# GAT blocks in a written order with their logits in PSUM, PSUM operands in the slot stage, and a fence between one-hots and GIN

## The chip, the core and the metric

The kernel runs on one core of one Trainium2 chip. Its metric is the time of one execution on the device in microseconds (us); the median of three runs is given. A run under the hardware profiler gives the trace and has a time of its own.

The core has five engines that run their own queues of instructions in order: PE (matrix multiplication; its weight loads are shown as PEld), DVE (VectorE), ACT (ScalarE), POOL (GpSimd) and SP (here only a queue that issues DMAs). They meet through semaphores. SBUF and PSUM are the memories on the chip[...].

## The reference

3125 nodes with 64 features and 103,125 edges, sorted by destination. Two parts, each added to its input:

```python
h = jnp.maximum(_layernorm(x, axis=-1), 0.0)
x = x + _L0_gnn_ref(h, edge_index, edge_weight, ...)    # GIN
h = jnp.maximum(_layernorm(x, axis=-1), 0.0)
x = x + _L1_gnn_ref(h, edge_index, node_vec, ...)       # GAT
```

The GIN part has three layers; the sums over edges are weighted:

```python
agg = jax.ops.segment_sum(x[src] * ew[:, None], dst, num_segments=x.shape[0])
h = jax.nn.relu((agg + x) @ w1 + b1) @ w2 + b2
```

The GAT part adds a time embedding (two dense layers over sines and cosines of `noise_labels`), and has three layers of 8 heads, of width 256, 256 and 128; per layer a softmax over the edges of each destination, a batch normalization, a parallel dense path and a SiLU:

```python
logits = leaky_relu(al_s[src] + al_d[dst], 0.2)         # [edges, 8]
e = jnp.exp(logits - segment_max(logits, dst)[dst])
alpha = e / segment_sum(e, dst)[dst]
out = segment_sum(alpha[:, :, None] * xw[src], dst)     # + bias
x = silu(batchnorm(out + x @ aw + ab))
```

A dense layer to 64 features ends it. All is fp32.

## The kernel before

Nodes are handled in NT = 25 tiles of P = 128 (NP = 3200). If a flag computed on the chip allows it, the path of class `Fast` runs, as here. Its stages, with lines of the kernel:

- `search` (L623) and `rank` (L711) find the row of edges of each destination and sort destinations by degree, so that each tile t of destinations has its own number of edge slots, `CAPS[t]` (64 down to 23, 857 in all). ACT's queue zero-fills the dense matrix `adj` in DRAM (40.96 MB).
- `slots` (L749). Its inner `weigh(t)` (L817) compares all pairs of a destination's slots to add up double edges: the wide operations L824 (`same`), L827 (`part`, with the fixed triangle `earlier` of L812), L828 (a sum), L833 and L834. `put(t)` (L836) writes slot columns into `adj`, one indirect DMA on POOL for each column (L943): 857 of them, in the order tiles 0 to 2, 3 to 7, then 50 scatters of tables, then tiles 8 to 24. Under these run, on DVE, the compares L866 and L869 with the maximum L870, which pick for each destination and each tile of sources at most one edge (`tops`, later `lane`), a series of match and maximum operations for the edges left over (`row`, at most 44 for a destination, `MORE[t]` per block t of 128), a second `rank`, and the flag.
- `fast` (L1290): layer norm, the embedding `embed` (L154; its `em_t` loads are on SP, its first DVE operation is L175, its last copy on ACT L188), `hots` (L923) and then three `gin` (L954). `hots` makes for each of 25 tiles a one-hot of the chosen edges: the comparison L929 of `lane` and `iota` on DVE, 25 transposes on PE, copies on ACT (L938), and a store of 800 KB on SP (L939).
- `gin` reads the whole of `adj` (122.9 MB over three layers) in 225 loads on SP (L973, eight buffers), and multiplies on PE (L977).
- `gat` (L991) three times. Its first part makes the transformed features in three bf16 parts (`split`), the attention terms and the dense path. `add_edges` (L1058) is the largest stage of the kernel, and has a loop over the 25 tiles. For each step t:
  - `gather(t+1, ...)` (L1071): 26 slots for each destination (25 from the one-hots `hot`, loaded on SP, and the node itself), by 78 bf16 matmuls into PSUM tiles `g`, two slots in each, copied by ACT into `rows` (L1079). It works in three parts, of 12, 12 and 2 slots.
  - `add_part` (L1102) on the three parts of tile t: `times` multiplies by `e` on DVE (L1100), the second half of the slots is added onto the first (L1105), and 6+6+1 matmuls with the identity add up the rest on PE into `pa1` (L1107). Then a copy on ACT (L1163) and a store.
  - where they are due (L1165), blocks of left-over edges: `others` (L1111) fetches on POOL a row `at` and `MORE[k]` rows `rows` from DRAM (L950, six buffers of 8 rows), and lets POOL scatter the result of an earlier block into `more` (L943). `add_others` (L1125) makes logits (L1128), `lrelu` (L206), exponentials (`exps`, L1180 to L1183, the exponential itself on ACT L1182), `times`, identity matmuls (L1139) and a copy (L1140).
  - `weigh(t+1)` (L1085): logits of the next tile's 26 slots (L1088, L1092), `lrelu`, `exps`.
- `close_rows` (L1185) joins the parts, with batch norm; `finish` (L278) ends the kernel.

The language's scheduler decides the order of each engine's queue from its own estimates; the order of the text is a starting point, not the result. It also places the semaphores. Pools of buffers (`bufs`) decide how far a producer may run ahead. In PSUM there is one pool `gat_ps` for a whole layer, with two buffers for most names.

## Time and profile before

| what | us |
|---|---|
| median of three runs | 5105.78 (5102.36 to 5115.34) |
| profiled execution, own time | 5023.04 |
| its span, first to last instruction | 5021.1 |
| puts into `adj`, first to last | 243 to 1497 |
| GIN with what stands beside it | 1503 to 1922 |
| GAT loops, layers 0, 1, 2 | 1003, 1004, 692 |
| between and around them | 90, 133, 114, 63 |
| busy: PE, DVE, ACT, POOL | 2248.5, 2020.8, 862.4, 2677.6 |
| mean granted TensorE clock | 0.729 |

The page cuts the span into 40 slices and gives each engine's busy share in tenths. A line of a list of waits reads: engine, operation and line that waited, what ended the wait, total us, number of times, longest. A line of a timeline reads: start, duration (of all that is joined in the line, xN), engine, line, operation, output and input, and in brackets the idle time before it and what ended that. A line of stretches has the bounds, the length, each engine's busy time with its number of instructions, the granted clock, the DMA share and GB/s.

### The profile page before, as it was taken

What the parts mean: (1) busy time and instruction counts of PE and PEld (TensorE: products, weight loads), DVE (VectorE), ACT (ScalarE), POOL (GpSimd) and SP (SyncE); (2) the same over time, 40 slices, a digit from 0 to 9 for tenths busy, and PEclk for the clock granted to TensorE, in tenths of its full rate; (3) what the DMA queues carried; (4) which work ended last, traced back from release to release, by engine and by line L of the source; (5) the groups of instructions that cost most, each with busy time, mean ns of one, the idle gap of its engine ahead of it and who ended that gap; (6) DMA issues with size and microseconds to landing.
All of it is one profiled execution on the core that took longest, in us unless ns stands there. A gap on an engine that the chain in (4) does not pass through costs nothing. (4 is left out here: it accounts for less than half of the span.)

```text
span 5021.1 us, 36988 instructions
## 1 busy us (share of the span) xinstructions
PE 2248.5 (45%) x13235; PEld 1675.1 (33%) x13235; DVE 2020.8 (40%) x3336; ACT 862.4 (17%) x1812; POOL 2677.6 (53%) x2350
## 2 busy tenths in 40 slices
PE   0000000000008997466765665547765655456465
PEld 0000000000003333355544544436554544455464
DVE  3599202000006103355554445345653544344345
ACT  0000000000006202212211213212221213112122
POOL 2488777777770000565575540565575540677762
PEclk9555555555559997778887877778877877677787
DMA  9100000000008993433232213432232224432222
GB/s 382 61 1 0 7 1 16 0 1 1 1 1 315 363 380 142 110 85 87 84 94 78 75 52 124 103 96 87 82 93 76 76 57 122 80 79 81 73 79 69
DMA packets 235781, 465.63 MB, mean 93 GB/s; under 512 B 102719, under 2 KB 145858, under 8 KB 232386
## 3 DMA queue, kind: packets, MB, share of 16 engines
q1 hardware_dynamic: 113606, 252.99, 14.4%
q0 software_dynamic: 89424, 157.97, 13.1%
q10 hardware_dynamic: 32556, 52.20, 2.8%
q8 instruction: 106, 1.74, 0.1%
q14 instruction: 89, 0.73, 0.1%
HBM read 363.97 MB, written 99.01 MB: 92 GB/s over the span
## 5 line engine op out<-in xcount | busy, mean ns | idle before, releaser
L950 POOL DMA_INDIRECT rows<-tab,idx x1200 | 1464.7, 1221 | 831.8 <-PE pa L1139 482.9
L943 POOL DMA_INDIRECT adj<-val,celli x857 | 922.0, 1076 | 296.2 <-issue 260.3
L1078 PE MATMUL g<-split,xt 128*128 128x264 bf16 (+1 forms) x3825 | 501.4, 288 | 604.0 <-ACT xt L1079 550.8
L1078 PEld LDWEIGHTS <-xt 128*128 128x128 bf16 x3825 | 379.5, 110 | 715.2 <-issue 634.1
L977 PE MATMUL pa<-adj_t,h 128*64 128x512 f32 (+1 forms) x1050 | 280.3, 562 | 664.5 <-DMA adj_t<-adj 663.8
L950 POOL DMA_INDIRECT at<-ald,perm x75 | 73.1, 975 | 913.2 <-DVE l L1092 533.8
L1079 ACT COPY xt<-g 128x528 f32<-128x528 f32 (+1 forms) x900 | 462.5, 526 | 528.8 <-PE g L1078 293.2
L1139 PE MATMUL pa<-rows,ident 128*128 128x256 f32 (+1 forms) x2400 | 504.4, 365 | 34.5 <-ACT o L1140 24.1
L1128 DVE TENSOR_TENSOR l<-rows,at 128x64 f32<-128x64 f32 (+4 forms) x180 | 38.7, 215 | 1171.3 <-DMA rows<-tab,idx 1127.9
L1139 PEld LDWEIGHTS pa<-rows,ident 128*128 128x128 f32 x2400 | 429.5, 207 | 83.9 <-ACT o L1140 32.0
L1107 PE MATMUL pa<-xt,ident 128*128 128x256 f32 (+1 forms) x1800 | 418.6, 386 | 81.6 <-DVE xt L1105 80.9
L1100 DVE TENSOR_TENSOR xt<-xt,e 128x3072 f32<-128x3072 f32 (+1 forms) x150 | 416.4, 2817 | 0.0
L1078 PE MATMUL g<-split,hot 128*128 128x264 bf16 (+1 forms) x1800 | 246.1, 297 | 351.8 <-ACT xt L1079 295.9
L1107 PEld LDWEIGHTS pa<-xt,ident 128*128 128x128 f32 x1800 | 336.9, 217 | 135.4 <-DVE xt L1105 83.3
L977 PEld LDWEIGHTS pa<-adj_t,h 128*64 128x64 f32 x1050 | 82.9, 137 | 810.1 <-issue 744.4
L1078 PEld LDWEIGHTS <-hot 128*128 128x128 bf16 x1800 | 185.2, 113 | 405.8 <-issue 364.9
L1100 DVE TENSOR_TENSOR rows<-rows,e 128x2048 f32<-128x2048 f32 (+8 forms) x180 | 289.3, 1632 | 0.0
L175 DVE TENSOR_SCALAR em_t<-em_t,wave 128x512 f32<-128x512 f32 (+1 forms) x7 | 3.6, 515 | 659.0 <-DMA em_t<-in_node_vec 658.9
L1182 ACT ACTIVATE e<-l 128x208 f32<-128x208 f32 (+17 forms) x150 | 51.5, 343 | 1183.9 <-DVE l L1181 1183.7
L1105 DVE TENSOR_TENSOR xt<-xt 128x1536 f32<-128x1536 f32 (+1 forms) x150 | 216.5, 1485 | 0.0
L182 PE MATMUL p<-em_k,L_gnn_te_w 128*128 128x512 f32 (+1 forms) x14 | 8.7, 709 | 446.9 <-ACT em_k L180 446.9
L182 PEld LDWEIGHTS p<-em_k,L_gnn_te_w 128*128 128x128 f32 x14 | 2.8, 228 | 451.6 <-issue 450.2
(255 smaller groups left out, 2552.2 us busy)
## 6 DMA issues: line engine op xcount, KB each, us to landing
adj_t<-adj SPq DMA_DIRECT2D x150, 512.0 KB, 7.1
adj_t<-adj SPq DMA_DIRECT2D x75, 576.0 KB, 8.0
xt<-hot SPq DMA_DIRECT2D x51, 800.0 KB, 4.6
adj<-zero ACTq DMA_DIRECT2D x25, 1600.0 KB, 32.8
hot<-by_src SPq DMA_DIRECT2D x25, 800.0 KB, 4.2
hot<-hot SPq DMA_DIRECT2D x24, 800.0 KB, 4.5
rows<-tab,idx POOLq DMA_INDIRECT x1200
adj<-val,celli POOLq DMA_INDIRECT x857
```

What stands on the lines that cost most here:

```text
L182: nc.tensor.matmul(p1[:, :w], w1, k, start=True, stop=True)
L943: st = self.nc.gpsimd.indirect_dma_start(out=table, out_offset=bass.IndirectOffsetOnAxis(ap=idx, axis=0), in_=row, in_offset=None)
L950: self.nc.gpsimd.indirect_dma_start(out=out, out_offset=None, in_=table, in_offset=bass.IndirectOffsetOnAxis(ap=idx, axis=0))
L977: nc.tensor.matmul(pa[i * D0 : (i + 1) * D0, c : c + w], h[:, s], tiles[i][:, c : c + w], start=s0 == 0, stop=s0 + i >= NT - 2 and i == 1,)
L1078: nc.tensor.matmul(g[:, j, :W], one, a[:, min(s, t) if s == NT else s], start=k == 0, stop=k == 2)
L1079: nc.scalar.copy(rows[:, i : i + 2], g[:, :, :W])
L1100: nc.vector.tensor_tensor(r, r, e[:, s0 : s0 + n, :, None].to_broadcast([P, n, H, C]), op=ALU.mult)
L1105: nc.vector.tensor_add(rows[:, :m, :D], rows[:, :m, :D], rows[:, m:n, :D])
L1107: nc.tensor.matmul(pa, self.ident, rows[:, j, :D], start=s0 + j == 0, stop=s0 + n == NS and j == m - 1)
L1128: nc.vector.tensor_tensor(l[:, k0 : k0 + n], rows[:, :n, D:], at[:, None, :].to_broadcast([P, n, H]), op=ALU.add)
L1139: nc.tensor.matmul(pa, self.ident, rows[:, k, :D], start=k0 + k == 0, stop=k0 + k == MORE[t] - 1)
L1182: nc.scalar.activation(e, l, AF.Exp)
```

## The change

Four parts.

1. In `slots`, ACT copies `src`, `wgt`, `order` (a row CMAX−k) and `key` to PSUM; the wide operations read one operand there. The triangle `earlier` goes: `part` is `same` times `order`, and its sum becomes a maximum that is compared with `order`. The PSUM tiles of `rank` have two buffers instead of four, which `pt1` shares.
2. In GAT, each layer's PSUM pool is split into three, one for each of its stages (three, one and three buffers by default, `g` two). The scatter of `more` leaves its group of independent writes (`group=None`), so each follows the one before it.
3. `add_edges` runs under `manual_schedule`: each engine gets its instructions in the order of the text. In this order `weigh(t+1)` stands before the blocks that are due; a block is due one step later; only the first part's second half is folded on DVE, so the identity matmuls are 6+12+2 for each tile. Logits and exponentials of `weigh` are in one PSUM tile (`le1`), those of a block in another (`le2`; for more than 32 rows the logits stay in SBUF); `lrelu` becomes `bend`, two operations instead of one.
4. `no_sync_barrier` between `hots` and `gin`: the scheduler does not move instructions over it. On SP's queue all `em_t` loads and the 25 stores of `hot` now stand before the first `adj_t` load.

```diff
@@ slots
-                pp = ps.tile([P, BLK], F32, name="pp", bufs=4)
+                pp = ps.tile([P, BLK], F32, name="pp", tag="pp", bufs=2)
...
-            earlier = sp.tile([P, CMAX, CMAX], F32, name="earlier")
...
+            src_p = ps.tile([P, NC], F32, name="src_p")
+            nc.scalar.copy(src_p, src)
+            wgt_p = ps.tile([P, NC + CMAX], F32, name="wgt_p")
+            nc.scalar.copy(wgt_p[:, :NC], wgt)
+            order = sp.tile([P, CMAX], F32, name="order")
+            nc.vector.tensor_scalar(order, k, -1.0, float(CMAX), op0=ALU.mult, op1=ALU.add)
+            nc.scalar.copy(wgt_p[:, NC:], order)
+            order_p = wgt_p[:, NC:]
...
-                    same, src[:, c, None].to_broadcast(wide), src[:, None, c].to_broadcast(wide), op=ALU.is_equal
-                )
-                nc.vector.tensor_tensor(part, same, earlier[:, :n, :n], op=ALU.mult)
+                    same, src[:, c, None].to_broadcast(wide), src_p[:, None, c].to_broadcast(wide), op=ALU.is_equal
+                )
+                nc.vector.tensor_tensor(part, same, order_p[:, None, :n].to_broadcast(wide), op=ALU.mult)
-                nc.vector.reduce_sum(again, part, axis=AX.X)
-                nc.vector.scalar_tensor_tensor(again, again, 0.0, taken[:, c], op0=ALU.is_equal, op1=ALU.mult)
+                nc.vector.reduce_max(again, part, axis=AX.X)
+                nc.vector.tensor_tensor(again, again, order_p[:, :n], op=ALU.is_equal)
+                nc.vector.tensor_tensor(again, again, taken[:, c], op=ALU.mult)
...
-                nc.vector.tensor_tensor(same, same, wgt[:, None, c].to_broadcast(wide), op=ALU.mult)
+                nc.vector.tensor_tensor(same, same, wgt_p[:, None, c].to_broadcast(wide), op=ALU.mult)
...
+            key_p = ps.tile([P, NC], F32, name="key_p")
+            nc.scalar.copy(key_p, key)
...
-                    u, key[:, None, c].to_broadcast(wide), ends[:, :, None].to_broadcast(wide), op=ALU.is_lt
-                )
-                nc.vector.tensor_tensor(u, u, key[:, None, c].to_broadcast(wide), op=ALU.mult)
+                    u, key_p[:, None, c].to_broadcast(wide), ends[:, :, None].to_broadcast(wide), op=ALU.is_lt
+                )
+                nc.vector.tensor_tensor(u, u, key_p[:, None, c].to_broadcast(wide), op=ALU.mult)
@@ gat
-            ps = ctx.enter_context(tc.tile_pool(name=f"gat_ps{layer}", bufs=2, space=PSUM))
...
+            with tc.tile_pool(name=f"gat_sum{layer}", bufs=2) as io, tc.tile_pool(
+                name=f"gat_ps_sum{layer}", bufs=1, space=PSUM
+            ) as ps, tc.manual_schedule():
                 self.add_edges(io, ps, layer, D, xt, yt, split, ald, stat, tab, ald_d, res, more)
@@ add_edges
+        def logits(name, n):
+            a = ps.tile([P, BLK], F32, name=name, tag=name)
+            half = BLK // 2
+            e = a[:, BLK - n * H :] if n * H > half else a[:, half : half + n * H]
+            l = io.tile([P, n * H], F32, name=f"l{name}", bufs=1) if n * H > half else a[:, : n * H]
+            return (v.rearrange("p (k h) -> p k h", h=H) for v in (l, e))
+
+        def bend(l, n):
+            z = io.tile([P, RMAX, H], F32, name="z")[:, :n]
+            nc.vector.tensor_scalar(z, l, SLOPE, None, op0=ALU.mult)
+            nc.vector.tensor_tensor(l, l, z, op=ALU.max)
...
             for s0, n, rows in now:
-                nc.vector.tensor_tensor(l[:, s0 : s0 + n], l[:, s0 : s0 + n], rows[:, :, D:], op=ALU.add)
-            self.lrelu(l, l)
+                nc.vector.tensor_tensor(
+                    l[:, s0 : s0 + n], rows[:, :, D:], ald[:, t, None, :].to_broadcast([P, n, H]), op=ALU.add
+                )
+            nc.vector.tensor_tensor(l, l, self.void[:, t, :, None].to_broadcast(wide), op=ALU.add)
+            bend(l, NS)
...
-            m = n // 2
-            nc.vector.tensor_add(rows[:, :m, :D], rows[:, :m, :D], rows[:, m:n, :D])
+            m = n // 2 if s0 == 0 else n
+            if m < n:
+                nc.vector.tensor_add(rows[:, :m, :D], rows[:, :m, :D], rows[:, m:n, :D])
...
-            late.append((more, [(o, self.perm[:, t : t + 1])], f"more{layer}"))
+            late.append((more, [(o, self.perm[:, t : t + 1])], None))
...
-            while done < NT and due[done] <= (t + 1) * due[-1] / NT:
+            if ahead:
+                now, e = nxt, weigh(t + 1, nxt)
+            while done < NT and due[done] <= t * due[-1] / NT:
                 add_others(done, *others(done))
                 done += 1
-            if more_:
-                now, e = nxt, weigh(t + 1, nxt)
@@ fast
                 k.hots(hp, k.ps)
+
+            tc.no_sync_barrier()
             for layer in (1, 2, 3):
                 k.gin(gp, io, layer, layer == 3, *h)
```

## The prediction

> **What bounds the kernel now.** I read the page's forty slices first, then stretches of the span, then the waits, then two timelines. The chain that ended last carries nothing here: 0% at every step.
>
> Three rows of the forty slices (125.5 us each):
>
> ```profile
> POOL 2488777777770000565575540565575540677762
> DMA  9100000000008993433232213432232224432222
> GB/s 382 61 1 0 7 1 16 0 1 1 1 1 315 363 380 142 110 85 87 84 94 78 75 52 124 103 96 87 82 93 76 76 57 122 80 79 81 73 79 69
> ```
>
> POOL alone works until slice 12 (the scatters into `adj`); then POOL stops and the DMAs run full for three slices (GIN); then three GAT layers in which nothing is full. The stretches, with busy time of PE, PEld, DVE, ACT, POOL, then clock, DMA share and GB/s; the last line is from a second question, inside GIN:
>
> ```profile
> 243.00:1497.00 1254.00, 10.99 (x19) 4.47 (x19) 321.90 (x913) 11.09 (x16) 977.52 (x907) 0.50 0.03 3
> 1503.00:1922.00 419.00, 376.41 (x2022) 159.62 (x2022) 108.96 (x91) 117.75 (x163) 0.00 (x0) 0.98 0.93 346
> 2012.00:3015.00 1003.00, 625.77 (x3407) 497.94 (x3408) 490.55 (x572) 223.48 (x431) 570.70 (x449) 0.80 0.30 82
> 4266.00:4958.00 692.00, 380.33 (x3398) 363.06 (x3395) 302.09 (x570) 144.68 (x427) 486.88 (x450) 0.75 0.30 75
> ...
> 1750.00:1875.00 125.00, 118.20 (x515) 44.90 (x512) 5.00 (x14) 7.86 (x14) 0.00 (x0) 1.00 0.98 378
> ```
>
> In the put stage 907 indirect DMAs take 1254 us. One undisturbed takes 0.965+0.305 = 1.27 us (0.96 to 0.97, and 0.30 of issue), 1154 in all, so about 100 us are lost. Where:
>
> ```profile
> 307.05 1.94 DVE L866 TENSOR_TENSOR under<-key,ends 128x825 f32<-128x825 f32 x2
> 307.98 3.71 POOL L943 DMA_INDIRECT adj<-val,celli  x1 [0.30 <-issue]
> 308.90 1.95 DVE L869 TENSOR_TENSOR under<-under,key 128x825 f32<-128x825 f32 x2
> 310.76 1.93 DVE L870 TENSOR_REDUCE tops<-under 128x25 f32<-128x825 f32 x2
> 312.00 0.97 POOL L943 DMA_INDIRECT adj<-val,celli  x1 [0.30 <-issue]
> ```
>
> A put that meets DVE reading two SBUF tensors ends only after it (3.71 us); the put beside the reduction does not (0.97).
>
> The waits of all engines, and the one on SP's queue:
>
> ```profile
> DVE l L1128 <- DMA rows<-tab,idx: 1127.9, 168, 14.3
> PE g L1078 <- ACT xt L1079: 846.7, 94, 47.6
> DVE em_t L175 <- DMA em_t<-in_node_vec: 658.9, 4, 655.2
> POOL rows L950 <- PE pa L1139: 482.9, 55, 19.8
> SPq L973 <- DMA adj<-val,celli: 656.5, 1, 656.5
> ```
>
> SP's first `adj_t` load waits 656 us for the puts, and behind it stand the small `em_t` loads and all stores of `hot`. One GAT step:
>
> ```profile
> 2645.77 0.21 DVE L1128 TENSOR_TENSOR l<-rows,at 128x48 f32<-128x48 f32 x1 [8.56 <-DMA rows<-tab,idx]
> 2660.05 3.12 POOL L950 DMA_INDIRECT rows<-tab,idx  x1 [12.79 <-PE pa L1139]
> 2685.97 0.21 DVE L1128 TENSOR_TENSOR l<-rows,at 128x48 f32<-128x48 f32 x1 [7.85 <-DMA rows<-tab,idx]
> 2688.22 4.12 PE L1078 MATMUL g<-split,hot 128*128 128x264 bf16 x18 [15.82 <-ACT xt L1079]
> ```
>
> This is a loop of two legs in series: 14.3 us from the logits to PE's release of a buffer, 25.9 from there through 19 indirect DMAs (24.1 by 1.27) to the next logits; 40.2 us, and 25 steps are the 1003. DVE waits for the newest rows with `weigh` and `times` behind it; ACT's exponential waits for DVE with the copies of `g` behind it; so PE stands 15.8 us.
>
> **The Trainium skill.** "SBUF — State Buffer", section "Who interferes with whom": a VectorE instruction with two SBUF inputs contends with GpSimd's reads, one with a single SBUF input outside the two-port modes does not, a reduction never. The trace agrees (3.71 against 0.97). "VectorE: DVE Perf Modes", section "The perf-mode tier table": fp32 tensor_tensor is at one element per cycle with SBUF or PSUM operands. The trace agrees for plain operands: the 512-wide op of L1225 with a PSUM input takes 686 ns, L1248 without 694. "TensorE: Matmul & The Clock Gate", Part 1: after an idle window of some 3.4 us PE is at half clock. Here gather matmuls come every 213 to 220 ns after the gaps, and every 112 when warm.
>
> **The change, part by part.**
>
> *Puts.* Losses by the DVE op that each stretched put meets: L827 21.9, L869 19.4, L824 16.7, L833 11.3 with 9.8 on the puts next to L828 and L834, L866 2.0; with small ones some 85. All get one PSUM operand: −85; bounds 60 and 95. Four ACT copies delay the first puts by about 2.5; the dropped `earlier` (4.4) stood early on DVE, under the work ahead of the first put, and gives nothing back (4.4 at most). `pp` with two buffers instead of four costs nothing: in the first `rank` a matmul takes about 0.9 and ACT's copy 0.58, so ACT keeps up; 8 copies not overlapped would be 5. But hots now run under the puts: the first two one-hots did so in the kernel before (842 and 847 us) and cost 3.23 each (the op is 3.49, both inputs SBUF), so 23 more cost +74 (58 if some fall between puts, 80 if none do). The embedding's two-SBUF ops (14 of 0.69) add some 4. Sum −5: the puts end near 1492.
>
> *Fence, GIN.* On SP `em_t` loads and 25 stores of `hot` now precede the first `adj_t` load, so embed and hots are done long before 1492. Moved out of GIN are 20 MB of stores, and ACT's and PE's share of hots. What remains is 3×40.96 = 122.9 MB; at the 378 GB/s of the pure stretch 325 us, with 6.5 to the first load (1496.7 to 1503.2 before) and, estimated, 5 of tail 337. End 1829 instead of 1917: −88 with the puts' −5. Bounds −65 (360 GB/s, as between 1625 and 1750 us) and −105. If hots were not done under the puts this gain is gone.
>
> *GAT, order.* `weigh(t+1)` and the tile's sums now stand before a block's rows on DVE, and a block is due a step later, so POOL fetches two blocks ahead: `rows` has six buffers of 8 rows, and a block takes two or three. Before, DVE weighted each block as it landed, while PE came to it only after its gather, and the buffers were all held by weighted blocks. POOL's 19×1.27 = 24.1 us per step then run beside the rest. The new loop is PE's and DVE's. PE: gather 78×0.112 = 8.7; identity sums 20×0.431 = 8.6 (two passes of some 0.2155; before 13, 5.6: the dropped fold is +3.0); other rows 16×0.431 = 6.9; together 24.3. PE then idles from the last gather to the first weighted rows: copy 0.6, `weigh` 3.1 (0.26, 0.26, 0.17, 0.37, twice 0.38 for the two ops of `bend`, 0.53, 0.38, exponential 0.38; what follows overlaps), the block's front 2.3, first `times` 2.3, less part of it under the last sums: 8.6. After that gap the clock is half for about 4 us: 2 lost. Sum 34.9 against 40.2. DVE waits on semaphores in 1097 instructions instead of 814, PE in 312 instead of 193; such an instruction has 21 ns on DVE, so 6 us in the kernel if none is hidden, which I leave to the range. DVE has 19.6 of work (490.55/25) less 2.2 of folds plus 0.3: 17.7, hidden. POOL's scatter of `more`, now dependent on the scatter before it, waits for a block's copy with the next fetches behind it, but those are two blocks ahead; without that slack it costs up to the 24.1 again.
>
> 25×34.9 = 872, first gather 10, three last blocks about 25: 907 a layer instead of 1003: −96, twice. Bounds −50 and −140. Layer 2 is half as wide; POOL's 450×1.27 = 571 is a floor, I take 622 instead of 692: −70. Between layers three PSUM buffers instead of two: −6; bounds −15 and +10 (pools closed between stages).
>
> *PSUM logits.* The same element counts; I take nothing. Bounds below zero (fewer SBUF conflicts with fetches, 1.30 against 0.95 us each, hidden now) and the rival below.
>
> Sum: −88−96−96−70−6 = −356 on the profiled execution's 5023 (span 5021): 4667. The median of the runs, 5106, lies 83 above; added, 4750.
>
> **The rivals.**
>
> *Only GIN gains.* POOL's scatter of `more` with its waits keeps rows late, and GAT steps stay near 40: 5106−88 = 5018. For: POOL is busy 570 us of a layer, its fetches take 1.30 us on average where DVE's two-input ops meet them, and it already waits 483 us for PE. Against: in the new loop POOL's 24 us need only be under 35, and even at 1.6 us for each of the 19 (30 us) they are.
>
> *Hots starve the puts.* Each one-hot of 3.49 us holds POOL for longer than it lasts (a put that starts just before it and one just behind, as the 3.71 above for two ops of 1.9): 23 times 2 us more, +45 over my sum, 4795. For: DVE is otherwise idle there, so the one-hots come as fast as the stores take them. Against: the two one-hots that the trace has cost 3.23.
>
> *PE stays warm*, front overlapped: −2 us over 62.5 full-step equivalents (25+25+12.5) is −125: 4625.
>
> *Slower.* `e` is read from PSUM with each element repeated over C; no row of before shows that. At half rate the 26×256+16×256 = 10,752 elements of a step take 11.2 us more; on the path, 62.5 steps give +700: 5450. It decides at 5.6 us per step (356/62.5 rounded), a factor of 1.5. Against: 686 against 694 ns.
>
> *The change does nothing:* the fence's loads stay behind `adj_t`. Against: the order of the new kernel's SP queue shows them ahead.
>
> **How the numbers follow.** My forecast 0.69, only GIN 0.11, starved puts 0.08, warm PE 0.07, slower 0.04, nothing 0.01. Measurement tells about 0.3% (15 us) apart. My case alone has 4680 to 4830; low takes in the warm PE, high the starved puts with half the layers' gain lost: 4630 to 4880, leaving out the two dearer rivals. Faster 0.94, same 0.02, slower 0.04.
>
> **What would show it.** Puts beside `weigh` and the key compares at 0.97, but stretched to about 4 us beside 23 one-hots around 800 to 1000 us; the last put near 1490; GIN at 378 GB/s for some 330 us; no wait of DVE for rows in GAT, POOL waiting for ACT's copy instead, and steps of 35 us with a PE gap of 8 to 9 us. Wrong: `times` slower than 3.35 us for 3072 elements, rows still waited for, or puts ending after 1530.

## The result, and the profile after

The changed kernel takes 5976.39 us (median, 5967.48 to 5989.8) against 5110.56 us of the kernel before, measured beside it: 1.1696 times, with a 95% interval of 1.1664 to 1.1728. It is 17% slower; 4750 was forecast.

One thing has to be said first, since no number below can be read without it. The measurements of this case are of two kinds, and all runs of one measurement, on one chip, are of the same kind. In one the kernel before takes 5100 to 5134 us and the changed one about 5976; in the other the kernel before takes 4980 to 5016 and the changed one about 4600. I call them the *late* and the *prompt* kind, for what the traces show in the first: counts on semaphores that arrive late. The result above is of the late kind. The profiled execution of before that the prediction was worked out from has a time of 5023.04, far from its own timed runs (5102 to 5115), and its trace shows no late counts, so it is of the prompt kind. Ratios are always to the kernel before within the same measurement, and stage times are compared within a kind or with the kind named.

The profile of the result has a span of 5987.8 us. Three rows of its forty slices (149.7 us each):

```profile
POOL 2574777777100213423333123333332223334332
DMA  9000000000399322222221342222221341211112
GB/s 365 7 1 5 1 21 11 11 11 11 137 384 382 113 53 68 66 60 65 60 63 45 106 106 62 64 66 61 67 65 49 95 86 50 52 46 47 51 38 61
```

The full-rate part of GIN now has two full slices (384 and 382 GB/s), with the stores of `hot` out of it, as forecast. But the GAT layers move 45 to 68 GB/s in most slices where before had 70 to 100, and POOL, at 5 to 7 tenths there before, is at 1 to 4. So everybody waits. The stretches, in the columns of the prediction: the puts, GIN, and the gathers of layers 0 and 2:

```profile
246.00:1533.00 1287.00, 63.97 (x286) 37.05 (x287) 379.63 (x979) 59.00 (x76) 946.05 (x907) 0.51 0.05 9
1631.00:1956.00 325.00, 305.75 (x1355) 119.06 (x1356) 12.87 (x36) 20.57 (x36) 0.00 (x0) 0.99 0.98 377
2050.00:3277.00 1227.00, 715.34 (x3614) 564.66 (x3614) 425.64 (x519) 222.48 (x413) 416.71 (x428) 0.77 0.24 63
4861.00:5873.00 1012.00, 434.08 (x3613) 407.27 (x3613) 275.99 (x518) 147.18 (x414) 408.61 (x428) 0.69 0.21 50
```

GIN takes the 325 us of the forecast's 122.9 MB at 378 GB/s. A gather of layer 0 takes 1227 us, and no engine has more than 716 of work in it. Stage by stage against the trace of before (which is prompt, so this is where the time is, not yet whose fault it is; the comparison within the late kind follows with the experiments): end of GIN +38, the three gathers +247, +234 and +339, the stretches between and after them +43, +33 and +32; together +967, the difference of the spans. What the engines wait for:

```profile
DVE le L1117 <- ACT xt L1093: 1635.9, 108, 65.6
POOL rows L959 <- PE pa L1166: 1078.7, 29, 111.6
ACT xt L1093 <- remote: 937.1, 127, 22.0
```

DVE waits for ACT's copies of the gathered rows, POOL for PE, and ACT (third line) for "remote": what ended its wait is not an instruction that had ended just then. ACT's copy L1093 needs only the matmuls of `g` ahead of it. One place in a step, all engines that matter:

```profile
2652.39 3.35 DVE L1127 TENSOR_TENSOR xt<-xt,le 128x3072 f32<-128x3072 f32 x1
2655.33 1.27 ACT L1093 COPY xt<-g 128x528 f32<-128x528 f32 x2 [0.30 <-PE g L1092]
2655.65 0.68 DVE L1127 TENSOR_TENSOR last<-last,le 128x512 f32<-128x512 f32 x1
2656.10 0.95 POOL L959 DMA_INDIRECT rows<-tab,idx  x1 [0.30 <-issue]
...
2661.44 1.51 PE L1092 MATMUL g<-split,xt 128*128 128x264 bf16 x12
...
2671.11 0.94 POOL L959 DMA_INDIRECT rows<-tab,idx  x1 [0.30 <-issue]
2672.35 1.00 POOL L951 DMA_INDIRECT gat_more<-o,perm  x1 [0.30 <-issue]
2672.56 0.60 ACT L1093 COPY xt<-g 128x528 f32<-128x528 f32 x1 [11.35 <-remote]
2673.21 1.48 PE L1092 MATMUL g<-split,xt 128*128 128x264 bf16 x6 [10.26 <-issue]
...
2677.47 1.10 ACT L1093 COPY xt<-g 128x528 f32<-128x528 f32 x2 [4.32 <-remote]
2678.12 4.12 PE L1092 MATMUL g<-split,xt 128*128 128x264 bf16 x18 [3.44 <-ACT xt L1093]
```

PE's twelve matmuls, two `g` tiles full, are over by the trace at 2662.95. ACT starts on the first at 2672.56 and PE, which has no buffer left, stands for 10.26 us. From 2650.6 POOL had been issuing one indirect DMA each 1.25 us or so; at first copies followed matmuls all the same (the second line), while DVE was at work. DVE's last operation ends at 2656.33, and after it DVE has one of 0.27 us; the first late count comes at 2666.91. The next pair is late again; then POOL pauses (its last DMA ends at 2674.63), and by 2678 copies follow matmuls at once.

The same thing appears where it is cleanest, among the one-hots, which the fence has brought under the puts. DVE's comparisons L936, one for each tile; each needs a buffer that the 25 transposes of a tile (L944) release:

```profile
1243.39 3.49 DVE L936 TENSOR_TENSOR oh<-lane,iota 128x3200 bf16<-128x3200 f32 x1 [66.52 <-PE pt L944]
1313.38 3.49 DVE L936 TENSOR_TENSOR oh<-lane,iota 128x3200 bf16<-128x3200 f32 x1 [66.50 <-PE pt L944]
...
1523.38 3.49 DVE L936 TENSOR_TENSOR oh<-lane,iota 128x3200 bf16<-128x3200 f32 x1 [66.50 <-PE pt L944]
1559.05 3.49 DVE L936 TENSOR_TENSOR oh<-lane,iota 128x3200 bf16<-128x3200 f32 x1 [32.17 <-PE pt L944]
1563.04 3.49 DVE L936 TENSOR_TENSOR oh<-lane,iota 128x3200 bf16<-128x3200 f32 x1 [0.49 <-PE pt L944]
```

They are 70.0 us apart, and 4.0 to 4.3 from 1559 on. POOL's last put ends at 1532.8, the last late count comes at 1557.7. ACT's copies of eight transposes (L945) inside one such tile:

```profile
915.78 1.01 ACT L945 COPY by_src<-pt 128x1024 bf16<-128x1024 bf16 x1 [20.63 <-remote]
938.18 1.01 ACT L945 COPY by_src<-pt 128x1024 bf16<-128x1024 bf16 x1 [21.39 <-remote]
960.58 1.01 ACT L945 COPY by_src<-pt 128x1024 bf16<-128x1024 bf16 x1 [21.39 <-issue]
963.39 0.27 ACT L945 COPY by_src<-pt 128x128 bf16<-128x128 bf16 x1 [1.80 <-PE pt L944]
```

22.40 us for eight transposes and 2.8 for one (960.58 to 963.39): 2.80 for each, 25 of them 70.0. By PE's own records a transpose starts every 0.107 us or so, and eight take 1.01. So each transpose adds 2.80 us to the time at which its group's count is seen, as if it were counted, or finished, at that pace. I call a PE count late if it reaches the waiting engine more than 1.2 us after the last matmul of its group has started. In this trace 508 of 4919 are late; in the trace of before that the prediction used, 2 of 4867, and these two, at the very end of the kernel, are in every trace. The others fall into stretches; each begins while POOL issues indirect DMAs or at most 6 us later. Each ends at most some 7 us after POOL's last one, with one exception, the 25 us after the last put just shown. There is none in GIN, where the DMAs move 377 GB/s and POOL does nothing.

### The profile page after: what moved, and what is told of

Same layout as the page of the kernel before. It is cut to its first block, busy times and chain, and to the rows that moved or that the text cites. A ratio compares the mean times of both kernels' runs of the same rounds, so it can differ in the third digit from the quotient of the medians.

```text
span 5987.8 us, 39493 instructions
## 1 busy us (share of the span) xinstructions
PE 2612.7 (44%) x14285; PEld 1976.4 (33%) x14285; DVE 1958.7 (33%) x3361; ACT 883.0 (15%) x1816; POOL 2330.5 (39%) x2350
## 5 line engine op out<-in xcount | busy, mean ns | idle before, releaser
L959 POOL DMA_INDIRECT rows<-tab,idx x1200 | 1157.7, 965 | 1435.9 <-PE pa L1166 1078.7
L1166 PE MATMUL pa<-rows,ident 128*128 128x256 f32 (+1 forms) x2400 | 606.9, 427 | 507.3 <-DVE rows L1127 447.0
L1166 PEld LDWEIGHTS pa<-rows,ident 128*128 128x128 f32 x2400 | 513.0, 250 | 601.0 <-DVE rows L1127 465.9
L1093 ACT COPY xt<-g 128x528 f32<-128x528 f32 (+1 forms) x900 | 467.8, 529 | 1487.7 <-remote 937.1
L1135 PE MATMUL pa<-xt,ident 128*128 128x256 f32 (+1 forms) x2700 | 586.2, 379 | 22.1 <-DVE xt L1133 22.1
L1135 PEld LDWEIGHTS pa<-xt,ident 128*128 128x128 f32 x2700 | 500.4, 218 | 82.3 <-DVE xt L1133 26.1
L1127 DVE TENSOR_TENSOR xt<-xt,le 128x3072 f32<-128x3072 f32 (+1 forms) x150 | 422.1, 2814 | 0.0
L944 PE MATMUL pt<-identb,oh 128*128 128x128 bf16 x625 | 77.6, 302 | 653.4 <-issue 534.9
L936 DVE TENSOR_TENSOR oh<-lane,iota 128x3200 bf16<-128x3200 f32 x25 | 87.3, 3491 | 646.4 <-PE pt L944 646.4
L944 PEld LDWEIGHTS <-oh 128*128 128x128 bf16 x625 | 65.3, 140 | 665.7 <-issue 664.3
L1127 DVE TENSOR_TENSOR rows<-rows,le 128x2048 f32<-128x2048 f32 (+8 forms) x180 | 284.3, 1628 | 0.0
L945 ACT COPY by_src<-pt 128x1024 bf16<-128x1024 bf16 x100 | 79.3, 828 | 649.0 <-remote 529.5
```

The costliest lines, as they stand in the source:

```text
L936: nc.vector.tensor_tensor(oh, self.lane[:, t, :, None].to_broadcast(wide), self.iota[:, None, :].to_broadcast(wide), op=ALU.is_equal)
L944: nc.tensor.transpose(pt[:, i], oh[:, s0 + i], self.identb)
L945: nc.scalar.copy(by_src[:, s0 * P : (s0 + n) * P], pt[:, :n].rearrange("p s d -> p (s d)"))
L959: self.nc.gpsimd.indirect_dma_start(out=out, out_offset=None, in_=table, in_offset=bass.IndirectOffsetOnAxis(ap=idx, axis=0))
L1093: nc.scalar.copy(rows[:, i : i + 2], g[:, :, :W])
L1127: nc.vector.tensor_tensor(r, r, e[:, s0 : s0 + n, :, None].to_broadcast([P, n, H, C]), op=ALU.mult)
```

## The experiments

The theories. *Order*: the written order or the fence is itself slow, whatever the chip does. *S*: counts are late where POOL issues indirect DMAs and DVE has been idle for some us, which the new order makes more of. *T*: they are late while POOL issues indirect DMAs, whatever DVE does, and the change puts more work that hands on through PE beside them. *PSUM*: logits and exponentials in PSUM collide with PE's writes. The expectations below call *T* R at first, and *Order* W, or I where this exact sequence of instructions is meant; P says that lateness belongs to the conditions of a measurement, and D that the traffic of the fetches makes it, whoever issues them.

### The fence alone, and all without it

```diff
 # fence alone: the kernel before with
+            tc.no_sync_barrier()
 # no fence: the changed kernel with
-            tc.no_sync_barrier()
```

> The kernel before with the fence alone. Seen in the changed kernel: while POOL issues indirect DMAs, PE needs 2.80 us for each bf16 transpose of the one-hot stage (0.107 elsewhere), and the one-hot stage of 25 tiles lasts until 1622 us. Theory S (PE is slow when POOL issues indirect DMAs and DVE has been idle for some us, in whatever kernel): the same here, some 70 us a tile, hots end near 1600 and GIN near 1930, median 5090 to 5140. Rival R (PE is slow beside POOL's indirect DMAs whatever DVE does): the same. Rival W (it comes from the written order and the PSUM tiles of the changed kernel): the one-hots are through by 1000 us, GIN ends near 1830, median near 5020.

> The changed kernel without the fence. S and R: the one-hots leave the puts and take 0.107 us a transpose again beside GIN; puts end near 1430, GIN near 1850 instead of 1956; GAT loops stay at 1226, 1214 and 1012 us with late PE results; median near 5870. W: GAT the same. If the one-hots under the puts had put PE into a state that lasts, GAT would come down to 900, 900 and 620, median near 4750.

The fence alone: 4983.0 against 4995.87 us, 0.9973 (0.9956 to 0.999). Without it the rest of the change takes 4610.39 us, 0.9215 (0.9169 to 0.9262). This measurement turned out to be of the prompt kind: both traces have the 2 late counts at the end and no others. With the fence alone GIN ends at 1884 instead of 1917 in the trace of before, but the puts last to 1548 instead of 1497 since one-hots now hold them. Without it, puts end at 1417 and GIN at 1837.

### Work for DVE where it was idle

```diff
 # hots: beside each comparison L936
+            for _ in range(5):
+                nc.vector.memset(idle, 0.0)         # [P, 2048], 1.765 us
 # the second kernel also in add_edges, each step: 7 after the parts,
 # 5 and 2 after the logits of parts 0 and 1
+                nc.vector.memset(idle, 0.0)         # [P, 1024], 0.912 us
```

> The changed kernel with five memsets of 2048 elements on DVE (some 2.2 us each, of a tile that nothing reads) for each of the 25 one-hot tiles. They do no useful work. S: while DVE runs them PE does its transposes at full rate, a tile takes some 15 us and the one-hots are through by about 1250 us; GIN then ends near 1830 to 1850, 110 us earlier; median near 5865. R and W: transposes stay at 2.8 us, the one-hots end near 1622, median near 5976.

> The same, and in GAT's loop memsets of 1024 elements on DVE (some 1.1 us each): seven after the products of a tile, five and two between the logits of its parts, where DVE otherwise waits for ACT's copies. S: the gather keeps its rate beside POOL's fetches, a step of layers 0 and 1 takes 35 to 38 us, GAT loops near 920, 920 and 650, median 4750 to 4900. R: GAT loops stay at 1226, 1214 and 1012 or grow, median 5870 to 6000.

4626.56 us, 0.9248 (0.9192 to 0.9304), and 4887.05 us, 0.9768 (0.972 to 0.9817). They were of the same prompt measurement, so they say nothing on S: there were no late counts to take away. The fillers only cost time: the one-hots come every 5.49 us instead of 4.27 and let one put through each, 25×1.22 = 31 us, and the puts end at 1522.5. No later run had fillers in a measurement of the late kind, so S was not put to this test.

### The changed kernel again

> The changed kernel itself once more. In the four runs just made, PE gave its results at the rate of its starts under the puts and in GAT's gathers, with the fence and without it, and in GAT without any filler, so DVE's idleness (theory S) isn't what slows it there. Theory P (the late PE results belong to the chip or to the conditions of the first measurement, not to the kernel's instructions): if it runs on the same chip as those four, PE isn't late, the one-hots are through by 1000 us, GAT loops take some 820, 820 and 550 us, median 4600 to 4640. Theory I (they belong to this exact sequence of instructions, which fence and fillers both disturb): late results again, 600 us for the one-hots and GAT loops of 1226, 1214 and 1012, median near 5850.

The same kernel in a later measurement: 4600.44 us against 5003.2, 0.9203 (0.9146 to 0.9261). Its trace has 2 late counts of 5147. The stretches that answer to those above:

```profile
246.00:1489.00 1243.00, 102.36 (x670) 71.96 (x670) 419.00 (x992) 106.75 (x140) 965.70 (x907) 0.51 0.07 20
1500.00:1825.00 325.00, 306.19 (x1358) 119.44 (x1359) 12.85 (x36) 20.56 (x36) 0.00 (x0) 0.99 0.97 377
1922.00:2745.00 823.00, 650.68 (x3615) 532.60 (x3615) 425.63 (x519) 223.16 (x412) 416.79 (x425) 0.90 0.35 93
3928.00:4477.00 549.00, 369.81 (x3617) 351.10 (x3617) 276.06 (x518) 146.03 (x415) 398.55 (x412) 0.84 0.38 90
```

DVE, ACT and POOL have the same work in a gather as in the result's trace (425.6, 223, 417 us), in 823 us instead of 1227. *Order* falls: the order is not slow as such. The two spans differ by 1390.1 us: GIN starts 131 later (1630.8 against 1500.2), the gathers are longer by 404, 395 and 464, and the rest, −3, is nothing.

### Which part is slow in the late kind

The kernel before with the hunk on `slots` alone (part 1), of which

```diff
-                    same, src[:, c, None].to_broadcast(wide), src[:, None, c].to_broadcast(wide), op=ALU.is_equal
+                    same, src[:, c, None].to_broadcast(wide), src_p[:, None, c].to_broadcast(wide), op=ALU.is_equal
```

and the kernel before with the hunks on `gat` and `add_edges` alone (parts 2 and 3), of which

```diff
+            ) as ps, tc.manual_schedule():
...
+            if ahead:
+                now, e = nxt, weigh(t + 1, nxt)
+            while done < NT and due[done] <= t * due[-1] / NT:
```

> The kernel before with the slot stage's PSUM operands alone. If the prediction's term for the puts holds, they end near 1415 instead of 1497 (the 85 us of stretched puts, less 2.5 for ACT's copies), GIN with the one-hots still inside takes its 415 us and ends near 1835, and the rest is as before: 80 us less, ratio 0.984. Should the chip be one on which PE's results come late beside POOL's indirect DMAs (theory P), nothing changes in that here, since PE does nothing under the puts.

> The kernel before with the GAT edits alone (written order, PSUM tiles, one fold instead of three, later blocks). On a chip without late PE results the gain of the changed kernel less that of puts and fence: GAT gathers of 820, 820 and 550 us instead of 980, 980 and 673, which with the joins between layers is some 310 us, ratio 0.938. On a chip with late results (theory P): gathers of 1226, 1214 and 1012, ratio 1.16.

These two were measured together, in the late kind. `slots` alone: 5122.79 against 5113.13 us, 1.002 (1.0009 to 1.0031). GAT's parts alone: 5970.11, 1.168 (1.1654 to 1.1707), as much as the whole change; its gathers take 1219, 1217 and 1008 us, and 412 of 4929 PE counts are late. With `slots` alone 184 of 4579 are, GIN ends at 1955, where the whole change has 1956, and the gathers take 976, 986 and 726.

No trace of the kernel before was taken in this kind, but the two traces hold its halves, with its own order on every engine: the one with GAT's parts alone up to the end of GIN (1951), the one with `slots` alone from there on. Put together they span 5117 us, where its runs had 5113. Against these halves the result has +5 up to the end of GIN, +250, +228 and +286 in the gathers, and +38, +33 and +30 between and after them, 871 in all; the medians in the result are 866 apart. So the 17% are GAT's. And before itself, against its prompt trace, has +33 up to the end of GIN, −3, +6 and +53 in the gathers: in the two wide layers its order loses next to nothing in this kind.

DVE is touched as well. In the kernel with GAT's parts alone, the series of maxima, under the puts:

```profile
402.33 0.20 DVE L880 MAX8 row<-key 128x8 f32<-128x39 f32 x1 [2.54 <-remote]
405.13 0.20 DVE L880 MAX8 row<-key 128x8 f32<-128x38 f32 x1 [2.60 <-remote]
408.63 0.20 DVE L880 MAX8 row<-key 128x8 f32<-128x37 f32 x1 [3.30 <-remote]
```

They wait for counts of DVE itself alone, 2.5 to 3.3 us; in the trace of before the same operations follow each other within some 0.2. The intervals here, 2.80 and 3.50, are multiples of 0.70. The part `slots` has no gain left in this kind. Its stretched puts cost 17 us, where those of before cost 98 in the prompt trace; but there is one wait of 63.8 us for DVE, and 367 puts follow each other in 1.40 instead of 1.27 us. They end at 1530, and at 1528 with the code of before, which has a wait of 50.9 us for DVE. Its expectation, that nothing would change here since PE has no work under the puts, was wrong.

### No indirect DMAs in the GAT loops

```diff
-            self.fetch(at, ald_d, self.perm[:, t : t + 1])
+            nc.sync.dma_start(at, ald_d[t * P : (t + 1) * P])
...
-                    self.fetch(rows[:, k], tab, self.idx[:, t, k0 + k : k0 + k + 1])
+                    nc.sync.dma_start(rows[:, k], tab[(k0 + k) % NT * P : ((k0 + k) % NT + 1) * P])
...
-                self.scatter(*late.pop(0))
+                nc.sync.dma_start(*late.pop(0))
```

The same bytes are moved by plain DMAs of SP, from and to other rows, so these kernels leave out the true sums over left-over edges and only their times count.

> The changed kernel with no indirect DMA on POOL inside the GAT loops: the rows of left-over edges, the row of destination terms and the store of a block go as plain DMAs of the same size on SP, from rows of tab that are not those of the edges, so the output is another. Theory T (on some chips an engine's semaphore counts come late, in steps of 0.70 us, while POOL issues indirect DMAs; the kernel before takes some 5110 us there and 5000 elsewhere): on such a chip no late PE results in GAT, gathers of 820, 820 and 550 us instead of 1226, 1214 and 1012, and late ones only under the puts; on the other chips the same 820, 820, 550, since POOL is off the path there. Rival D (it is the traffic of the fetches into SBUF, not who issues it): on such a chip late results in GAT as before, 1200 us a layer.

> The changed kernel without indirect DMAs in the GAT loops once more (plain DMAs of the same size on SP, other rows, so another output), for a chip with late counts: theory T expects gathers of 820, 820, 550 us there and late PE results only under the puts; rival D some 1200 a layer. On another chip 820, 820, 535 again.

> The changed kernel without indirect DMAs in the GAT loops, once more for a chip with late counts (plain DMAs of other rows, so another output): theory T expects gathers of 820, 820, 550 us there and late PE results only under the puts; rival D some 1200 a layer. On another chip 820, 820, 535 again.

> The changed kernel without indirect DMAs in the GAT loops, once more for a chip with late counts (plain DMAs of other rows, so another output): theory T expects gathers of 820, 820, 550 us there and late PE results only under the puts; rival D some 1200 a layer. On another chip 820, 820, 535 again.

The first three were of the prompt kind: 4570.29 against 4992.16 us, 0.9154 (0.9122 to 0.9186), and one run each of 4563.06 (before 4985.63) and 4568.72 (before 5001.69). They show the base line: plain DMAs make next to no difference there (gathers 822.5, 823, 532). The fourth, one run, is of the late kind, with before at 5126.7: **4704.27 us, 0.918**. Its stretches of one-hots and of the first gather, and its longest "remote" wait:

```profile
892.00:1625.00 733.00, 78.50 (x625) 65.96 (x623) 80.34 (x23) 79.25 (x100) 500.79 (x466) 0.50 0.10 27
2054.00:2875.00 821.00, 648.15 (x3611) 530.93 (x3611) 425.54 (x519) 223.51 (x413) 0.00 (x0) 0.90 0.31 94
...
ACT by_src L945 <- remote: 554.4, 26, 22.9
```

In one and the same execution the one-hots beside POOL's puts are as late as in the result (892 to 1625 us; copies wait 554 us), and the gathers, with POOL empty, are as short as in the prompt kind: 821, 823 and 531 us. Late counts: 75 of 5158, none in the loops; apart from the two at the end, all come before 1561 us, 25 us after the last put. So without POOL's indirect DMAs beside them the loops lose nothing, and *D* falls: the same bytes by SP's plain DMAs do no harm. Whether it takes POOL as the issuer or an indirect DMA isn't told apart, since the edit changes both. Measured beside it, the kernel of the next experiment keeps POOL's indirect DMAs, and its gathers take 1106, 1109 and 992.

*S* doesn't fall by this run, since it too needs POOL's indirect DMAs, and the traces speak for it. Take the PE counts from the first gather to the last where POOL's indirect DMAs fill more than half of the 2.5 us around the start of the last matmul, and sort them by DVE's work in the next 1.2 us. In the result's trace 393 of 987 are late where DVE works less than a fifth of that time, and 5 of 351 where it works more than four fifths. With `slots` alone, which has the order of before, it is 103 of 822 and 26 of 1159. An idle DVE can be an effect of late counts as well as their condition, and no run in the late kind changed DVE's work alone: this is not shown.

### Logits in SBUF

```diff
-            a = ps.tile([P, BLK], F32, name=name, tag=name)
...
+            e = io.tile([P, BLK], F32, name=f"e{name}", bufs=1)[:, : n * H]
+            l = io.tile([P, BLK], F32, name=f"l{name}", bufs=1)[:, : n * H]
```

> The changed kernel with the logits and exponentials of GAT in SBUF again; order, fold and the rest stay. The prediction took nothing for PSUM: the products by e then hold POOL's fetches (two SBUF inputs), which are off the path; 4600 within 15 us, ratio 0.920. If the PSUM operand cost DVE anything, faster; if the held fetches came onto the path, slower by up to 0.35 us for each of 1200 rows, 420 us.

In the late kind, in the measurement of the run just told: 5796.81 us, 1.1318 (1.1246 to 1.139), gathers 1106, 1109 and 992, 423 of 4941 counts late. PSUM operands are not what makes counts late. Against the result's own gathers (1227, 1214, 1012, another measurement) a tenth is gone in two layers, which this run doesn't explain. The 4600 us that were expected are for the prompt kind, in which it was not measured.

### One-hots with an operand in PSUM

```diff
+        iota_p = ps.tile([P, P], F32, name="iota_p", bufs=1)
+        nc.scalar.copy(iota_p, self.iota)
...
-                oh, self.lane[:, t, :, None].to_broadcast(wide), self.iota[:, None, :].to_broadcast(wide), op=ALU.is_equal
+                oh, self.lane[:, t, :, None].to_broadcast(wide), iota_p[:, None, :].to_broadcast(wide), op=ALU.is_equal
```

with a PSUM pool of its own for the stages ahead of GIN.

> The changed kernel with the one-hot comparison of the hot stage reading iota from PSUM. On a chip without late counts: the 25 comparisons no longer hold the puts (74 us in the prediction, 70.6 measured as 1487.7 less 1417.1), the puts end near 1418, GIN at full DMA rate near 1755 and the whole near 4530. On a chip with late counts: one-hots still 70 us a tile, puts near 1530, 5970. Rival: the comparison holds POOL with any operand, puts end near 1488, time as the changed kernel's.

4526.84 against 4992.16 us, 0.9062 (0.9033 to 0.9092), prompt. First the changed kernel, measured again, then this one; a put beside a one-hot:

```profile
837.29 3.49 DVE L936 TENSOR_TENSOR oh<-lane,iota 128x3200 bf16<-128x3200 f32 x1 [0.77 <-PE pt L944]
837.66 3.96 POOL L951 DMA_INDIRECT adj<-val,celli  x1 [0.30 <-issue]
```

```profile
879.73 3.49 DVE L938 TENSOR_TENSOR oh<-lane,iota_p 128x3200 bf16<-128x3200 f32 x1 [0.78 <-PE pt L946]
880.73 0.97 POOL L953 DMA_INDIRECT adj<-val,celli  x1 [0.30 <-issue]
882.00 0.97 POOL L953 DMA_INDIRECT adj<-val,celli  x1 [0.30 <-issue]
```

The operation itself is no slower, and the puts end at 1415 instead of 1488. The one-hots had held the puts for some 73 us; the prediction's term was 74.

### The scheduler's order, and both

```diff
-            ) as ps, tc.manual_schedule():
+            ) as ps:
```

> The changed kernel with the scheduler's order in the GAT loops instead of the written one; the text, PSUM tiles and single fold stay. If the gain of GAT comes from the written order (the prediction: DVE meets a block's rows after the next tile's logits), gathers fall back to some 960, 960 and 660 us, and the whole is near 4960 on a chip whose kernel before takes 5000. If the order of the text is enough for the scheduler, 820, 820, 550 and 4600. On a chip with late counts (kernel before near 5110) anything that keeps POOL's fetches off the gathers is faster than the written order: below 5976.

> The changed kernel with the scheduler's order in GAT and the one-hot comparison reading iota from PSUM, together. On a chip without late counts the two gains are in different stages and add: 4515 less 73 is 4442, ratio 0.890 (a_nomanual 0.905, a_oh_psum 0.906). On a chip with late counts (kernel before near 5110): one-hots 70 us a tile under the puts whatever their operands, GAT late again since POOL's fetches run beside gathers here too; 5700 to 6000.

All of the change but the written order: 4514.72 against 4985.63 us, 0.9051 (0.903 to 0.9072), prompt. So the written order (0.9203) loses some 1.5% of the time of before to the scheduler's, with the same operations. PE around the sums of a block's rows (L1166), first in the written order, then in the scheduler's:

```profile
2309.93 1.03 PE L1135 MATMUL pa<-last,ident 128*128 128x256 f32 x4
2318.94 9.95 PE L1166 MATMUL pa<-rows,ident 128*128 128x256 f32 x36 [7.98 <-DVE rows L1127]
2328.72 4.56 PE L1092 MATMUL g<-split,xt 128*128 128x264 bf16 x36
```

```profile
2323.71 1.03 PE L1135 MATMUL pa<-last,ident 128*128 128x256 f32 x4
2324.58 6.43 PE L1092 MATMUL g<-split,xt 128*128 128x264 bf16 x48
2330.85 7.96 PE L1166 MATMUL pa<-rows,ident 128*128 128x256 f32 x36
```

PE's 7.98 us for the weighted rows are filled with the next gather, and the 36 sums then run in 7.96 us instead of 9.95. With the one-hots' operand in PSUM as well: 4447.72 against 5001.69 us, 0.8896 (0.8874 to 0.8918).

### The dropped fold put back

```diff
-            m = n // 2 if s0 == 0 else n
+            m = n // 2
```

on the kernel with both.

> The faster variant (scheduler's order in GAT, iota from PSUM) with the fold of all three parts on DVE again, 13 instead of 20 identity sums a tile. The prediction priced the dropped fold at 3.0 us of PE a step and called DVE's 2.2 hidden. If PE is the bound of a step as it says, 62.5 steps of 3.0 give up to 187 us back, 4260, ratio 0.853; if DVE or the handshakes bind now, nothing: 4448, 0.890; if the folds delay the sums, up to 62.5 times 2.2 more, 4585. On a chip with late counts (kernel before near 5110): between 5200 and 5900, since the scheduler's order leaves POOL's fetches beside the gathers.

> The same kernel as a_best_fold once more, to see it on a chip with late counts: there (kernel before near 5110) 5200 to 5900 if POOL's fetches beside the gathers are what costs; on another chip 4326 again.

Prompt: 4326.27 against 4990.86 us, 0.8662 (0.8629 to 0.8695); the gathers are 712, 714 and 557 instead of 777, 774 and 565. Late: 5365.06 against 5133.51, 1.0455 (1.0425 to 1.0486), gathers 979, 978 and 836, 512 of 4730 counts late. So the best version in the one kind still loses in the other. In the late kind no version that computes the whole of the reference beat the kernel before.

## Why the prediction was wrong

**The step that failed** is the one on GAT's order: "POOL's 19×1.27 = 24.1 us per step then run beside the rest". It prices that overlap at the durations of the trace of before, as if what PE hands on were not touched by fetches beside it. In the kind of measurement that the result is of, it is: counts come microseconds after their matmuls (2.80 us for each transpose, 9.2 us at the worst in the step shown), and the loop waits where I had overlap. The gathers take 1227, 1214 and 1012 us, where the order of before has 976, 986 and 726 in the same kind, the forecast had 907, 907 and 622 for the whole loops, and without POOL's indirect DMAs they take 821, 823 and 531.

Why the order of before is spared is known in part. It is not that POOL and PE take turns there: in its loop of layer 0 the two are busy together for 384 us of 1003 (POOL with its 0.3 us between DMAs). What the change makes more of is PE at work beside POOL while DVE does nothing: 133 us of that loop before, 323 us of the 823 of the changed kernel's gather in its prompt trace. That is what S asks for; no run has tested it.

The fence moved the one-hots beside the puts in the same way: the first `adj_t` load stands at 1626.5 us, where the forecast had 1498.5, and the forecast's −88 at the end of GIN became +38 against the trace of before and +5 within the late kind. That end is the same without the fence (`slots` alone), so the fence gave back what it won.

**The 83 us** between the profiled execution and the median were added as if they were a constant. They were the only sign in the data shown that the runs and the trace were of different kinds: 5023 against 5102 to 5115, where the runs themselves agree to 0.3%. The prediction gives no reason for them. None of the rivals, the slower one included, has late counts in it.

**In the prompt kind the steps can be checked one by one**, on the changed kernel measured again against the trace of before:

| step | forecast | measured |
|---|---|---|
| puts end at | 1492 | 1488.3 |
| end of GIN | −88 | −93 |
| layer 0, from start of gather to the next | −96 and a share of −6 | −119 |
| layer 1 | −96 and a share of −6 | −128 |
| layer 2 to the end | −70 | −86 |
| the span | −356 | −423 |

- *Puts.* Right, term by term: the key compares and `weigh` no longer stretch puts (0.97 us beside them; without the fence the puts end 80 us earlier, at 1417), and the one-hots hold them for about as long as computed. (The second of the two one-hots that the 3.23 us are read from starts at 854.6 us, not 847, and 907×1.27 is 1152; neither changes the sum.) The Trainium skill, "SBUF — State Buffer", section "Who interferes with whom", lets a VectorE instruction with one SBUF input run beside GpSimd's reads; the PSUM operand for `iota` shows it with 0.97 against 3.96 us.
- *Fence, GIN.* Right at the place named, 324 us at 377 GB/s. But the fence pays for it: the one-hots it moves, which the forecast has under the puts, delay these by 73 us. The changed kernel without the fence has 0.9215, with it 0.9203; the intervals don't part them.
- *GAT.* Right in sign, in the loop named and in the length of a step: from the third step on the mean is 34.9 us in layer 0 and 34.8 in layer 1, and 34.9 was forecast. The gap of 8.6 us is 7.98 in the step shown, and the 2 us for the clock after it are there too (9.95 against 7.96 us for the 36 sums, whose first eight or so come 0.427 us apart instead of 0.216). The layers gain more than forecast at their start: the first two steps take 12 and 25 us, and the sum had 25 whole ones.
- *The dropped fold*, +3.0 us a step, 187 for 62.5 steps: measured on another order, 4447.72 to 4326.27 (two measurements), about 120. Right in sign, too dear there; on the written order it wasn't measured.
- *PSUM logits at nothing, the slower rival at 11.2 us a step.* `times` has 3.35 us for 3072 elements in both kernels. Here a repeated operand in PSUM costs no more than one in SBUF.

**Still open**: why some measurements are late and others prompt. The number of the chip doesn't settle it (one number gave both), and time of day wasn't separated. Whether the engines finish late or only their counts arrive late isn't settled either: the Trainium skill, "Perfetto Trace Analysis", section "Tensor Engine Instruction (MATMUL, LD_WEIGHTS)", says that a matmul's reported end is an estimate and that its semaphore update is pushed after PSUM has acknowledged the data. The trace agrees as far as it goes: starts of transposes are 0.107 us apart while their counts come at 2.80, so an end in the record proves nothing here. Open too are DVE's part (S) and why late counts went on for 25 us after the last put. The tenth that logits in SBUF took off a late gather was not pursued.

## What to carry to other kernels

A duration from a trace holds for the neighbours and for the measurement that it had there: the trace of before shows PE and POOL busy together for 384 us of a loop without a late count, and yet the overlap of the new order cost 228 to 286 us a layer in the kind of measurement that the result is of. When the profiled execution and the timed runs differ by more than the runs among themselves, find out why before adding the difference to a sum. Where GpSimd issues long series of indirect DMAs, hand-offs through PE in small pieces beside them are a risk that one measurement may not show; so compare orders in several.

## What the runs showed of the hardware

- In some measurements, while GpSimd issues indirect DMAs (one each 1.25 to 1.27 us), counts of other engines can arrive late, in steps that fit 0.70 us: 2.80 us for a bf16 transpose (starts 0.107 apart), 2.80 and 3.50 between maxima on DVE that wait for DVE's own counts. Beside such DMAs 393 of 987 PE counts in the result's GAT loops were late with DVE idle and 5 of 351 with DVE at work. It ended at most 7 us after the last such DMA, once 25. In GIN, with DMAs of the hardware queues at 377 GB/s and GpSimd idle, no count was late.
- The same kernel has 5976 and 4600 us by the kind of measurement, the kernel before 5110 and 5000: which of the two is faster depends on it.
- A put meeting a one-hot with two SBUF operands took 3.96 us, and 0.97 with one of them in PSUM, at the same 3.49 us for the one-hot.
